# A fused attention and expert kernel: the opening of its first stage in another order

## The chip, the cores and the metric

The kernel runs on one core of one Trainium2 chip. Its time is the device time of one launch, in microseconds (us). The core has five engines that run side by side, each through its own list of instructions: PE (TensorE, matrix products), DVE (VectorE), ACT (ScalarE), POOL (GpSimd) and SP (SyncE, which here only issues transfers). POOL issues transfers as well, on a queue of its own. Engines wait for each other and for transfers by semaphores, and an engine never runs an instruction ahead of an earlier one that still waits.

## The reference

Four layers follow each other, each added to its input: an attention layer whose context is summed by a decaying scan, a layer with 16 experts of which 6 are taken per row, a cross attention under a mask, and a layer with 2 experts of which 1 is taken. Only the first layer and the mask concern this change.

```python
# x: 32 x 56 x 256, ctx_2048: 32 x 1500 x 256, mask: 32 x 1500
def _L0_xattn_ref(Z, kv, decay, W_in, b_in, W_out, b_out, gamma, beta):
    K = jax.nn.sigmoid(decay)
    x = jnp.einsum('btd,ed->bte', kv, W_in) + b_in
    def scan_fn(s, xt):
        s = K * s + xt
        return (s, s)
    _, states = lax.scan(scan_fn, s0, jnp.swapaxes(x, 0, 1))
    proj = jnp.einsum('btd,ed->bte', states, W_out) + b_out
    summary = jnp.mean(proj, axis=1, keepdims=True)
    y = Z + summary
    mu = jnp.mean(y, axis=-1, keepdims=True)
    var = jnp.mean((y - mu) ** 2, axis=-1, keepdims=True)
    return (y - mu) / jnp.sqrt(var + LN_EPS) * gamma + beta
...
x = x + _L0_xattn_ref(_layernorm(x), ctx_2048, ...)
x = x + _L0_ffn_ref(_layernorm(x), ...)                      # 16 experts, 6 per row
x = x + _L1_xattn_ref(_layernorm(x), ctx_2048, mask)         # masked cross attention
x = x + _L1_ffn_ref(_layernorm(x), ...)                      # 2 experts, 1 per row
```

The mean over all states is one weighted sum over the 1500 context rows: row t counts with 1 + K + ... + K^(1499 - t). So the first layer needs, for each of the 32 elements of the batch, one weighted sum of 1500 rows of 256 numbers, and the two weight matrices can be multiplied together once.

## The kernel before, in words

The batch is taken in 16 pairs of elements. A pair's 112 rows of x stand in 128 partitions (56 rows, 8 empty, 56 rows, 8 empty), which is why `xr`, the tile with all rows, is set to zero before the rows are loaded.

**Loads.** Context elements pass through a ring of five slots (`ring`, 1536 KB each). SP loads slots 0 to 4 at the start, with a chunk of four pairs' rows of x (two transfers of 224 KB) after each of the first four. Each call of `count_in(b)` (L315) ends by issuing the load of element b + 5 into the slot that it has read (L331). POOL issues the weights and, last, the mask (L259 to L265), 46.9 KB.

**Constants.** DVE scans the decay into `crow` (L282). Twelve PE products with one column each turn it into columns (`cr`, L292), one more reverses it with `flip` (L299), and DVE copies make `cz`, the weights of the sums (L301 to L306). `count_in(0)` and `count_in(1)` then make the sums of the first pair on PE (L325, 24 products each). PE multiplies the two weight matrices (L341, L349), and makes the bias row and `takes` (L357 to L379). DVE then builds `iota` and the tables `i99` and `om` for the later sort of rows by expert (L389 to L402), and the statistics of the first four pairs (`first_stats(0)`, L425). POOL forms `z` and adds `bet` to `xr` for pairs 0 and 1 (`first_rows(0)`, L432 and L436).

**Mask analysis.** In front of the loop DVE finds for each element where the seen positions begin and whether they fit a window of 384 (L612 to L635): a scan that numbers the positions, two reductions over position times mask, one sign turn of the positions between them, and ten small operations. The results, `starts` and `bad`, are read in the later stages. All its operands lie in parts of `w0_sb`, the tile that later holds the weights of the 16 experts.

**The loop.** Round p does, in this order of issue: `first_norm(p - 1)` and `residual(p - 1)` on DVE (L471 to L479), the sums of pair p, `sum_out` (an ACT copy, L440), the sums into columns (`sp`, PE, and `sv`, DVE, L446 and L451), the projection (`sT`, `sm`, L459 and L463), for pair p - 1 the second normalisation on POOL (`xn`, L491), the turn on PE (L195), the gate (L505) and the choice of experts (`best`, DVE, L516 to L523), and `to_rows(p)` (`bp`, L467), which round p + 1 needs. For earlier pairs it counts places (L537 to L559) and sorts (L571, L593). Rounds 0 to 2 also make four further pairs' statistics (`first_stats(4 * p + 4)`, L425). POOL makes the next `z` and `xr` rows: two pairs in round 0, then one pair a round in the order z, xr, xn. Four buffers hold z, so the fifth z waits until `residual(0)` has used the first.

**What sets the order.** PE, DVE, ACT and SP run their instructions in the order in which the code issues them. In this stage POOL's order is arranged by the framework. After the loop come the 95 expert blocks, the cross attention and the 15 blocks of the last layer, which this change leaves as they are.

The call in question, as it stands in the loop:

```python
            if p >= 1:
                residual(p - 1)
                count_in(2 * p)
                count_in(2 * p + 1)
            sum_out(p)
```

Of the kernel before, what the change touches and what calls it, by code (L numbers as in the profile page):

```python
# [8 lines left out]
F32 = mybir.dt.float32  # L9
U8 = mybir.dt.uint8  # L10
# [3 lines left out]
ALU = mybir.AluOpType  # L14
AX = mybir.AxisListType
# [4 lines left out]
P = 128  # L20
# [39 lines left out]
def xattn_ffn_kernel(  # L60
# [52 lines left out]
    V.tensor_reduce(  # L113
        valid, ident.rearrange("p (h s) -> p h s", s=64)[:, :, 0:S], AX.XY, ALU.add
    )
    row = const.tile([P, 1], F32, name="row")
    V.tensor_reduce(row, before, AX.X, ALU.add)
    V.tensor_scalar(row, row, -1.0, float(P - 1), ALU.mult, ALU.add)
# [14 lines left out]
    V.tensor_scalar(i128, i128, float(P), None, ALU.mult)  # L133

    xr = const.tile([P, NP, D], F32, name="xr")
    G.memset(xr, 0.0)
    gw0_sb = const.tile([P, KD, E0], F32, name="gw0_sb")
    gw1_sb = const.tile([P, KD, E1], F32, name="gw1_sb")
    sel = const.tile([P, NP, E0], F32, name="sel")
# [63 lines left out]


    A.preload_act_table_set("natural_log_exp_and_others")
    w0p = ctx.enter_context(ExitStack())
    w0_sb = w0p.enter_context(tc.tile_pool(name="w0", bufs=1)).tile([P, E0, W0], F32, name="w0_sb")

    def load_w0_up():
        for m, w in ((0, wg0), (1, wu0)):  # L210
# [23 lines left out]
    with tc.tile_pool(name="p1", bufs=1) as p1, tc.tile_pool(name="p3", bufs=3) as p3, tc.tile_pool(  # L234
# [6 lines left out]
        xv = x.rearrange("(p h) s d -> h s p d", h=2)  # L241
        for i in range(NRING):
            load_ctx(i, slots[i])
            if i < 4:
                for h in range(2):
                    nc.sync.dma_start(
                        out=xr[64 * h : 64 * h + S, 4 * i : 4 * i + 4, :],
                        in_=xv[h][:, 4 * i : 4 * i + 4, :],
                    )
        p0 = p1x.enter_context(ExitStack())  # L250
        pw0 = p0.enter_context(tc.tile_pool(name="p0", bufs=1))
# [3 lines left out]
        bout_sb = p1.tile([1, D], F32, name="bout_sb")  # L255
        gam = p1.tile([P, D], F32, name="gam")
        bet = p1.tile([P, D], F32, name="bet")
        for sb, w in ((win_sb, w_in), (wout_sb, w_out), (bin_sb, b_in), (bout_sb, b_out)):
            nc.gpsimd.dma_start(out=sb, in_=w)  # L259
        for sb, w in ((gam, gamma.partition_broadcast(P)), (bet, beta.partition_broadcast(P))):  # L260
            nc.gpsimd.dma_start(out=sb, in_=w)
        for sb, w in ((gw0_sb, gw0), (gw1_sb, gw1)):
            nc.gpsimd.dma_start(out=sb, in_=w)
        mrow = w0_sb[0:B, 4, 0 : T // 4].bitcast(U8)
        nc.gpsimd.dma_start(out=mrow, in_=mask)  # L265

# [16 lines left out]
            crow, kd[:, 3:4].to_broadcast([1, T]), ones[0:1, 0:1].to_broadcast([1, T]), 0.0,  # L283
            ALU.mult, ALU.add,
        )
        ccol = p1.tile([P, NCH], F32, name="ccol")
        cz = p1.tile([P, NCH, Q + 1], F32, name="cz")
        G.memset(cz, 0.0)
# [17 lines left out]
            V.memset(cz[0:q, JM * m + r : JM * m + JM, 1:2], 0.0)  # L306
        sel2 = p1.tile([P, Q], F32, name="sel2")
        V.tensor_reduce(sel2, ident.rearrange("p (g b) -> p b g", b=Q), AX.X, ALU.add)

        pend = {}  # L310

# [74 lines left out]
        for l in range(NL):  # L386
# [7 lines left out]
        V.tensor_reduce(  # L394
            om[:, 1:2], ident.rearrange("p (g o l) -> p g o l", o=2, l=NLP)[:, :, 1, :], AX.XY,
            ALU.add,
        )
        V.tensor_scalar(om[:, 0:1], om[:, 1:2], -1.0, 1.0, ALU.mult, ALU.add)
        for o in range(2):
            V.tensor_scalar(om[:, 2 + o : 3 + o], om[:, o : o + 1], 0.5, -0.5, ALU.mult, ALU.add)  # L400
        for o in (1, 0):
            V.tensor_scalar(  # L402
                i99[:, o, :], i99[:, 0, :], om[:, o : o + 1], om[:, 2 + o : 3 + o], ALU.mult, ALU.add
            )
# [203 lines left out]
        at_t = w0_sb[0:B, 0:2, :].rearrange("p a b -> p (a b)")[:, 0:T]  # L608
        seen = w0_sb[0:B, 2:4, :].rearrange("p a b -> p (a b)")[:, 0:T]
        ends = w0_sb[0:B, 5, 0:4]  # L610
        turns = w0_sb[0:B, 6, 0 : 4 * Q].rearrange("p (i q) -> p i q", q=Q)
        V.memset(turns, 0.0)  # L612
        V.tensor_tensor_scan(
            at_t, ones[0:B, 0:1].to_broadcast([B, T]), ones[0:B, 0:1].to_broadcast([B, T]), 0.0,
            ALU.mult, ALU.add,
        )
        V.tensor_tensor_reduce(
            out=seen, in0=at_t, in1=mrow, scale=1.0, scalar=0.0, op0=ALU.mult, op1=ALU.max,
            accum_out=ends[:, 0:1],
        )  # L620
        V.tensor_scalar(at_t, at_t, -1.0, float(SPAN + 1), ALU.mult, ALU.add)
        V.tensor_tensor_reduce(
            out=seen, in0=at_t, in1=mrow, scale=1.0, scalar=0.0, op0=ALU.mult, op1=ALU.max,
            accum_out=ends[:, 1:2],
        )
        V.tensor_scalar(ends[:, 2:3], ends[:, 1:2], -1.0, float(SPAN), ALU.mult, ALU.add)
        V.tensor_scalar(turns[:, 0, 0:1], ends[:, 2:3], float(LATE), None, ALU.min)
        V.tensor_scalar(
            turns[:, 1, 0:1], ends[:, 0:1], turns[:, 0, 0:1], float(WIN), ALU.subtract, ALU.is_gt
        )  # L630
        for i in range(2):
            V.transpose(out=turns[:, 2 + i, :], in_=turns[:, i, :])
        V.tensor_copy(starts, turns[0:1, 2, :])
        V.tensor_reduce(turns[0:1, 0, 0:1], turns[0:1, 3, :], AX.X, ALU.max)
        V.tensor_copy(bad, turns[0:1, 0, 0:1])  # L635

        def some_pieces(n):
            for _ in range(n):
# [1045 lines left out]
```

## Time and profile before

| what | value |
|---|---|
| median of 3 runs | 731.97 us (731.27 to 733.47) |
| the profiled execution's own time | 731.96 us |
| its span, first to last instruction | 730.3 us |
| mean granted clock of PE | 0.954 |
| busy, whole span: PE, DVE, ACT, POOL | 90%, 55%, 33%, 48% |
| busy, 0 to 15 us: PE, DVE, ACT, POOL | 3.52, 5.62, 1.49, 11.01 us |
| busy, 30 to 45 us: PE, DVE, ACT, POOL | 3.15, 13.94, 1.42, 11.68 us |
| share of the transfer engines, 30 to 45 and 45 to 60 us | 0.97 and 0.67 |
| context moved into the ring | 32 loads of 1536 KB |

The profile lists each instruction with its start, its duration, its engine and its line in the kernel, and for each engine what ended its idle time. "acc<-ring,cz" means that the tile acc was written from the tiles ring and cz. A product in fp32 stands as two records, so 24 products are "x48". PEld is the loading of a product's fixed operand, which runs beside PE. The profile's names leave out numbers: `w_sb` is `w0_sb` here.

### The profile page before, as it was taken

The page shows a single profiled execution, that of the slowest core. Times are in us where ns is not written, and L with a number is a line of the kernel's source. Part 1 is how long each engine was busy: PE and PEld are TensorE (multiplying, and loading weights), DVE is VectorE, ACT ScalarE, POOL GpSimd, SP SyncE. Part 2 cuts the span into 40 slices and gives each one's busy share as a digit, 9 for nine tenths or more (in the row PEclk, how much of TensorE's full clock was granted, in tenths as well). Part 3 has the DMA queues.
Part 4 walks back from the last instruction along what each step waited for, and adds up shares of the span by engine and source line. Part 5 has one row for each costly group of instructions (what it writes and reads, how often), then busy time and mean ns, then how long its engine had stood idle before and what let it go on. Part 6 is the DMA issues. An engine that isn't in the chain of part 4 may idle for free.

```text
span 730.3 us, 13508 instructions
## 1 busy us (share of the span) xinstructions
PE 655.7 (90%) x4099; PEld 438.6 (60%) x4099; DVE 401.3 (55%) x1378; ACT 241.5 (33%) x704; POOL 349.5 (48%) x440
## 2 busy tenths in 40 slices
PE   3558988888779999999999999999988999999996
PEld 3424555555447777667777776666654666666664
DVE  3578687878824655534454447677876232322322
ACT  0113233333214444444444443566551111111110
POOL 6265455554344357667776776568342202112111
PEclk9869799999669999999999999999999999999999
DMA  8969899999716899645554554695941201011000
GB/s 259 316 271 391 316 364 356 369 358 315 214 50 203 265 334 286 206 138 144 153 155 136 157 160 131 185 313 108 332 149 53 69 9 44 25 36 39 26 30 18
DMA packets 70656, 136.62 MB, mean 187 GB/s; under 512 B 7731, under 2 KB 43204, under 8 KB 70580
## 3 DMA queue, kind: packets, MB, share of 16 engines
q1 hardware_dynamic: 56036, 100.31, 39.9%
q0 software_dynamic: 14544, 35.37, 18.0%
q8 instruction: 38, 0.62, 0.4%
q14 instruction: 38, 0.31, 0.1%
HBM read 109.54 MB, written 26.77 MB: 187 GB/s over the span
## 4 chain that ended last, share of the span: by engine, by line
PE 77%; DVE 11%; ACT 3%; POOL 2%; issue 2%; DMA 1%; POOLq 0%; DVEq 0%
PE gu L785 29%; PE y L812 18%; PE acc L325 7%; PE tp L803 5%; PE tp L195 4%; PE tp L913 2%; PE sp L1142 2%; PE owned L593 2%; PE bp L467 1%; PE op L1177 1%; PE lp L505 1%; POOL xn L491 1%; PE sT L459 1%; DVE st L183 1%; ACT xT L197 1%
## 5 line engine op out<-in xcount | busy, mean ns | idle before, releaser
L785 PE MATMUL gu<-w_sb,xT 128*128 x380 | 130.8, 466 | 3.4 <-ACT xT L197 1.9
L791 ACT ACTIVATE sg<-gu 128x176 f32<-128x176 f32 (+1 forms) x155 | 53.1, 343 | 230.3 <-PE gu L785 227.9
L943 POOL DMA_INDIRECT xb<-xn,idx x95 | 91.2, 960 | 63.1 <-PE tp L195 39.7
L785 PE MATMUL gu<-ring,xT 128*128 x240 | 113.7, 597 | 0.0
L797 DVE SCALAR_TENSOR_TENSOR hs<-sg,wgt,gu 128x176 f32<-128x176 f32 x95 | 37.7, 397 | 119.8 <-ACT sg L791 119.8
L812 PE MATMUL y<-w_sb,hT 88*128 x380 | 97.9, 380 | 0.0
L785 PEld LDWEIGHTS gu<-w_sb,xT 128*128 128x128 f32 x380 | 71.5, 191 | 30.7 <-ACT xT L197 2.9
L856 POOL DMA_INDIRECT g<-ys,early x78 | 74.8, 959 | 29.1 <-issue 15.3
L795 DVE TENSOR_TENSOR hs<-sg,gu 128x256 f32<-128x256 f32 x60 | 25.2, 421 | 112.3 <-ACT sg L791 112.3
L1428 POOL DMA_INDIRECT out<-ob,ti x15 | 14.8, 989 | 126.8 <-DVE ob L1425 126.5
L803 PEld LDWEIGHTS tp<-ident,hs 128*88 128x88 f32 (+1 forms) x310 | 40.0, 129 | 57.9 <-issue 46.9
L812 PEld LDWEIGHTS y<-w_sb,hT 88*128 88x128 f32 x380 | 64.5, 190 | 5.7 <-issue 0.6
L785 PEld LDWEIGHTS gu<-ring,xT 128*128 128x128 f32 x240 | 45.6, 192 | 33.3 <-issue 30.4
L805 DVE COPY hT<-tp 88x256 f32<-88x256 f32 (+1 forms) x155 | 64.3, 415 | 0.2 <-PE tp L803 0.2
L812 PE MATMUL y<-ring,hT 128*128 x240 | 61.7, 380 | 0.0
L197 ACT COPY xT<-tp 128x256 f32<-128x256 f32 x126 | 46.9, 372 | 43.4 <-PE tp L195 35.3
L803 PE MATMUL tp<-ident,hs 128*88 128x128 f32 (+1 forms) x310 | 59.2, 273 | 0.0
L325 PE MATMUL acc<-ring,cz 128*32 128x256 f32 x768 | 54.7, 442 | 0.2 <-DVE cz L301 0.2
L951 ACT COPY yb<-y 128x256 f32<-128x256 f32 x95 | 35.3, 372 | 42.8 <-PE y L812 41.9
L432 POOL TENSOR_SCALAR z<-xr,mva,rsa 128x256 f32<-128x256 f32 x16 | 23.0, 1437 | 49.6 <-DVE xr L479 45.4
L195 PE MATMUL tp<-ident,xb 128*128 128x128 f32 x220 | 42.5, 275 | 2.4 <-issue 2.4
L812 PEld LDWEIGHTS y<-ring,hT 128*128 128x128 f32 x240 | 41.0, 190 | 3.3
(307 smaller groups left out, 996.7 us busy)
## 6 DMA issues: line engine op xcount, KB each, us to landing
ring<-in_cx SPq DMA_DIRECT2D x32, 1536.0 KB
ys<-yb SPq DMA_DIRECT2D x95, 128.0 KB
ring<-in_cx SPq DMA_DIRECT2D x16, 384.0 KB
extra<-in_cx SPq DMA_DIRECT2D x16, 384.0 KB
xs<-zrow SPq DMA_DIRECT2D x5, 771.0 KB
w_sb<-in_wg SPq DMA_DIRECT2D x2, 1408.0 KB
w_sb<-in_wu SPq DMA_DIRECT2D x2, 1408.0 KB
xn<-xn SPq DMA_DIRECT2D x16, 128.0 KB
```

The costliest lines, as they stand in the source:

```text
L195: PE.transpose(tp[:, k * P : (k + 1) * P], xn[:, k * P : (k + 1) * P], ident)
L197: A.copy(xT.rearrange("p k c -> p (k c)"), tp[:, 0 : KD * P])
L325: PE.matmul(acc[Q * g : Q * g + Q, 0:D], lhsT=cz[:, j, 1 - h : 1 - h + Q], rhs=c[:, j, :], start=(h == 0 and m == 0), stop=(h == 1 and m = ...
L785: PE.matmul(gu[:, 0 : 2 * fp], lhsT=xT[i][:, k, :], rhs=w[:, bass.ds(at[i] + (u * piece + k * 2 * fp), 2 * fp)], start=(k == 0), stop=(k = ...
L791: A.activation(sg, gu[:, 0:fp], AF.Silu)
L797: V.scalar_tensor_tensor(hs[i, u], sg, wgt[:, i : i + 1], up, ALU.mult, ALU.mult)
L803: PE.transpose(tp[0:h, c * P : (c + 1) * P], a[:, c * h : (c + 1) * h], ident)
L805: V.tensor_copy(hT[i, u], tp[0:h, 0 : 2 * P])
L812: PE.matmul(y[i][:, 0:D], lhsT=a[:, c * P : (c + 1) * P], rhs=w[0:h, bass.ds(at[i] + (u * piece + doff + c * D), D)], start=(u == 0 and c ...
L856: G.indirect_dma_start(out=g, out_offset=None, in_=ys0[0 : n * P, :], in_offset=bass.IndirectOffsetOnAxis(ap=at[:, p, k : k + 1], axis=0),)
L943: G.indirect_dma_start(out=xb, out_offset=None, in_=xn0, in_offset=bass.IndirectOffsetOnAxis(ap=idx[:, i : i + 1], axis=0),)
L951: A.copy(yb, y[:, 0:D])
```

## The change

The arithmetic stays the same; only the order of the beginning changes, and products are added whose result nothing reads.

- The scan that numbers the positions becomes one of DVE's first instructions. The first reduction and the sign turn follow the decay scan, in front of the copies that wait for `cr`. The second reduction and the small operations follow `sel2`, in front of `cs`.
- The mask's transfer is now the first on POOL's queue.
- `xr` is set to zero later, after the other constants, and each chunk of rows is issued one ring load later, so that two context loads go ahead of the first rows.
- Seven products of `ident` with a row of ones, 128 x 512 each, stand at the head of PE's list, in front of `cr`.
- `count_in(2)` and `count_in(3)` move in front of the loop, behind `takes`; round 1 no longer has sums. `sum_out(0)` moves in front of `first_stats(0)`.
- `i99` and `om` are made in round 2, between `first_stats(12)` and `best(1)`.

```diff
@@ after valid
+    at_t = w0_sb[0:B, 0:2, :].rearrange("p a b -> p (a b)")[:, 0:T]
+    V.tensor_tensor_scan(
+        at_t, ones[0:B, 0:1].to_broadcast([B, T]), ones[0:B, 0:1].to_broadcast([B, T]), 0.0,
+        ALU.mult, ALU.add,
+    )
...
     xr = const.tile([P, NP, D], F32, name="xr")
-    G.memset(xr, 0.0)
...
     A.preload_act_table_set("natural_log_exp_and_others")
+    G.memset(xr, 0.0)
...
             load_ctx(i, slots[i])
-            if i < 4:
+            if i > 0:
                 for h in range(2):
                     nc.sync.dma_start(
-                        out=xr[64 * h : 64 * h + S, 4 * i : 4 * i + 4, :],
-                        in_=xv[h][:, 4 * i : 4 * i + 4, :],
+                        out=xr[64 * h : 64 * h + S, 4 * i - 4 : 4 * i, :],
+                        in_=xv[h][:, 4 * i - 4 : 4 * i, :],
                     )
...
+        mrow = w0_sb[0:B, 4, 0 : T // 4].bitcast(U8)
+        nc.gpsimd.dma_start(out=mrow, in_=mask)
         for sb, w in ((win_sb, w_in), (wout_sb, w_out), (bin_sb, b_in), (bout_sb, b_out)):
             nc.gpsimd.dma_start(out=sb, in_=w)
...
-        mrow = w0_sb[0:B, 4, 0 : T // 4].bitcast(U8)
-        nc.gpsimd.dma_start(out=mrow, in_=mask)
@@ behind the scan of the decay (crow)
+        V.memset(turns, 0.0)
+        V.tensor_tensor_reduce(
+            out=seen, in0=at_t, in1=mrow, scale=1.0, scalar=0.0, op0=ALU.mult, op1=ALU.max,
+            accum_out=ends[:, 0:1],
+        )
+        V.tensor_scalar(at_t, at_t, -1.0, float(SPAN + 1), ALU.mult, ALU.add)
+        for i in range(7):
+            warm = ps.tile([P, 512], F32, tag="ps", name="warm")
+            PE.matmul(
+                warm, lhsT=ident, rhs=ones[:, 0:1].to_broadcast([P, 512]), start=True, stop=True
+            )
...
         V.tensor_reduce(sel2, ident.rearrange("p (g b) -> p b g", b=Q), AX.X, ALU.add)
+        V.tensor_tensor_reduce(
+            out=seen, in0=at_t, in1=mrow, scale=1.0, scalar=0.0, op0=ALU.mult, op1=ALU.max,
+            accum_out=ends[:, 1:2],
+        )
...
+        V.tensor_copy(bad, turns[0:1, 0, 0:1])
...
         V.tensor_copy(takes, tk[0:3, 0:P])
+        for b in range(2, 4):
+            count_in(b)
...
-        V.tensor_scalar(i99[:, 0, :], iota[:, 0:NB0], -float(NOT), None, ALU.add)
...
+        def table_constants():
+            V.tensor_scalar(i99[:, 0, :], iota[:, 0:NB0], -float(NOT), None, ALU.add)
...
+        sum_out(0)
         first_stats(0)
         first_rows(0)
...
-        V.memset(turns, 0.0)
...
-        V.tensor_copy(bad, turns[0:1, 0, 0:1])
@@ in the loop
                 residual(p - 1)
+            if p >= 2:
                 count_in(2 * p)
                 count_in(2 * p + 1)
-            sum_out(p)
             if p >= 1:
+                sum_out(p)
                 second_root(p - 1)
...
                 first_stats(4 * p + 4)
+            if p == 2:
+                table_constants()
             if p >= 1:
                 best(p - 1)
```

More of the change, by code (lines that the diff above doesn't have):

```diff
@@ L115, in xattn_ffn_kernel @@
     )
+    w0p = ctx.enter_context(ExitStack())
+    w0_sb = w0p.enter_context(tc.tile_pool(name="w0", bufs=1)).tile([P, E0, W0], F32, name="w0_sb")
+    at_t = w0_sb[0:B, 0:2, :].rearrange("p a b -> p (a b)")[:, 0:T]
[3 more added lines that the diff above has]
+    )
     row = const.tile([P, 1], F32, name="row")
@@ L205, in xattn_ffn_kernel @@
     A.preload_act_table_set("natural_log_exp_and_others")
-    w0p = ctx.enter_context(ExitStack())
-    w0_sb = w0p.enter_context(tc.tile_pool(name="w0", bufs=1)).tile([P, E0, W0], F32, name="w0_sb")
+    G.memset(xr, 0.0)
     def load_w0_up():
@@ L285, in xattn_ffn_kernel @@
         )
+        seen = w0_sb[0:B, 2:4, :].rearrange("p a b -> p (a b)")[:, 0:T]
+        ends = w0_sb[0:B, 5, 0:4]
+        turns = w0_sb[0:B, 6, 0 : 4 * Q].rearrange("p (i q) -> p i q", q=Q)
+        V.memset(turns, 0.0)
[9 more added lines that the diff above has]
+            )
         ccol = p1.tile([P, NCH], F32, name="ccol")
@@ L308, in xattn_ffn_kernel @@
         V.tensor_reduce(sel2, ident.rearrange("p (g b) -> p b g", b=Q), AX.X, ALU.add)
+        V.tensor_tensor_reduce(
+            out=seen, in0=at_t, in1=mrow, scale=1.0, scalar=0.0, op0=ALU.mult, op1=ALU.max,
+            accum_out=ends[:, 1:2],
+        )
+        V.tensor_scalar(ends[:, 2:3], ends[:, 1:2], -1.0, float(SPAN), ALU.mult, ALU.add)
+        V.tensor_scalar(turns[:, 0, 0:1], ends[:, 2:3], float(LATE), None, ALU.min)
+        V.tensor_scalar(
+            turns[:, 1, 0:1], ends[:, 0:1], turns[:, 0, 0:1], float(WIN), ALU.subtract, ALU.is_gt
+        )
+        for i in range(2):
+            V.transpose(out=turns[:, 2 + i, :], in_=turns[:, i, :])
+        V.tensor_copy(starts, turns[0:1, 2, :])
+        V.tensor_reduce(turns[0:1, 0, 0:1], turns[0:1, 3, :], AX.X, ALU.max)
+        V.tensor_copy(bad, turns[0:1, 0, 0:1])
         pend = {}
@@ L391, in xattn_ffn_kernel @@
         i99 = p2.tile([P, 2, NB0], F32, name="i99")
-        V.tensor_scalar(i99[:, 0, :], iota[:, 0:NB0], -float(NOT), None, ALU.add)
         om = p2.tile([P, 4], F32, name="om")
[L394 to L403, printed above, removed]
-            )
+        def table_constants():
+            V.tensor_scalar(i99[:, 0, :], iota[:, 0:NB0], -float(NOT), None, ALU.add)
+            V.tensor_reduce(
+                om[:, 1:2], ident.rearrange("p (g o l) -> p g o l", o=2, l=NLP)[:, :, 1, :], AX.XY,
+                ALU.add,
+            )
+            V.tensor_scalar(om[:, 0:1], om[:, 1:2], -1.0, 1.0, ALU.mult, ALU.add)
+            for o in range(2):
+                V.tensor_scalar(om[:, 2 + o : 3 + o], om[:, o : o + 1], 0.5, -0.5, ALU.mult, ALU.add)
+            for o in (1, 0):
+                V.tensor_scalar(
+                    i99[:, o, :], i99[:, 0, :], om[:, o : o + 1], om[:, 2 + o : 3 + o], ALU.mult, ALU.add
+                )
         vals = p2.tile([P, NE * P], F32, name="vals")
@@ L605, in xattn_ffn_kernel @@
         pieces = list(w0_down_pieces())
[L608 to L611, printed above, removed]
-        V.memset(turns, 0.0)
[L613 to L634, printed above, removed]
-        V.tensor_copy(bad, turns[0:1, 0, 0:1])
         def some_pieces(n):
```

## The prediction

> **What bounds the kernel now.** I began with the busy slices. From 230 us on PE is nine tenths busy and the edit leaves that code alone, so only the first 205 us, the loop over 16 pairs, can move. There I read the windows of 2 us, columns PE, PEld, DVE, ACT, POOL, clock, DMA share, GB/s:
>
> ```profile
> 42.00:44.00 2.00, 1.59 (x4) 0.34 (x4) 1.86 (x11) 0.00 (x0) 2.00 (x2) 0.50 0.87 358
> 44.00:46.00 2.00, 1.55 (x7) 0.62 (x10) 0.45 (x2) 0.77 (x3) 1.75 (x3) 0.50 0.40 158
> 46.00:48.00 2.00, 2.00 (x20) 0.86 (x24) 1.70 (x5) 0.50 (x2) 0.00 (x0) 0.50 0.00 0
> 48.00:50.00 2.00, 1.96 (x32) 0.86 (x24) 0.91 (x3) 0.00 (x0) 1.51 (x2) 0.87 0.13 29
> ```
>
> The transfers run dry for some 5 us: the ring has no free slot because PE has not consumed elements 2 and 3. The waits of the first 60 us say why:
>
> ```profile
> ACT sm L463 <- PE sT L459: 13.6, 3, 10.9
> PE cr L292 <- DVE w_sb L282: 11.5, 1, 11.5
> ...
> PE sT L459 <- DVE sv L451: 8.4, 3, 7.9
> ...
> DVE ccol L297 <- PE cr L292: 5.9, 1, 5.9
> ```
>
> PE waits 7.9 us for one tiny DVE copy (sv), and everything behind it waits too. The chain of waits names what stood in front of it (start, duration, what):
>
> ```profile
> 39.01 1.73 DVE w_sb L622 x2
> ...
> 42.22 0.15 DVE sv L451
> ...
> 44.73 1.22 PE bp L467 x2
> 45.95 4.06 PE acc L325 x48
> ...
> 54.41 2.73 PE acc L325 x48
> ...
> 63.02 4.06 PE acc L325 x48
> ```
>
> So the mask analysis (L612 to L635, 32.53 to 42.2) sits on the path. After it the loop is no transfer problem: adding up the trace's DMA packets by queue, each context load lands 10 to 18 us before its sums from element 4 on. A round is a latency chain, DVE first_norm and residual, POOL z, xr and xn, PE turn, gate and bp, of 9.2 us (94.99, 104.19, 113.37 in the chain). Hence time won before round 2 reaches the end.
>
> **What the skill says.** "TensorE: Matmul & The Clock Gate", Part 1: the array's clock is half by default, full after a busy window of about 3.4 us, and the windows run free. The trace agrees: 48 products of L325 take 4.06 us at clock 0.50 and 2.73 at 1.00. The first clock event is at 21.2 us; before it the page prints 1.00, but the 40 products from 19.13 on run at the slow pace, so I take PE as slow until then. "SBUF — State Buffer", section on two separate sides: a DVE operation with two SBUF inputs and a POOL operation that reads SBUF exclude each other. The trace agrees: under the scan of L613 (to 35.84) the first z took 3.56 us, later ones 1.21:
>
> ```profile
> 32.63 3.21 DVE L613 TENSOR_TENSOR_SCAN w_sb<-ones 32x1500 f32<-32x1500 f32 x1
> ...
> 33.31 3.56 POOL L432 TENSOR_SCALAR z<-xr,mva,rsa 128x256 f32<-128x256 f32 x1 [4.20 <-ACT rsa L190]
> ```
>
> "DMA: Bandwidth & Descriptors", "Issuing engines are not separate DMA queues": POOL's and SP's transfers interleave on the same 16 engines; so they do here, the mask's packets ending between 17.1 and 20.5 us among the ring's.
>
> **The change, step by step.** Times of after carry a prime; sums are against the profiled execution, 731.96 us (span 730.3), which is the runs' median, 731.97.
>
> 1. Position scan first on DVE. It runs 1.83' to 5.05' (3.21 us as L613). POOL's affine_select for "before" reads SBUF, so by the lock it slips from 2.1' to 5.05'; the row reduction starts at 5.4' against 5.44 now. The decay scan ends at 11.3 as now. Price 0, hidden in DVE's 3.62 us wait; gain 0. The other end, no lock: 0.4 us gained and step 3 starts 3 us sooner.
>
> 2. Context before rows, and xr's memset later. Behind the affine_select the 3.50 us memset ends at 8.85'. SP holds two ring loads before the first rows, 3072 KB, which at before's pace land by about 14', so the engines have work until SP is released. Bytes are equal. Element 3 is preceded by two row chunks instead of three and lands near 29' (30.5 now). Rows come one chunk later: about 17', 24', 31', 37', needed at about 29', 32', 38', 55'. Price 0.
>
> 3. Mask first on POOL's queue. Issue 8.9'. The first POOL transfer now takes 2.85 us from issue (5.72) to first packet (8.57); so 11.8', landed about 12.4'. The weights issue 3.2 us later, from 9.4'; w_in lands about 14', its use is at 21'. The last of the nine waits for the mask to land, then come flip and cz.
>
> 4. Mask analysis in DVE's waits. The first reduction follows the landing: 12.4' + 1.97 + 1.17 for the sign turn = 15.5', then ccol. The rest, 1.73 + 1.5 us, stands before cs, idle now from 19.6 to 25.6. Flip's select is locked out until 15.5', ready 15.8'.
>
> 5. Seven unread products. One 128x512 fp32 product took 2.06 us at half clock (L583, 193.86) and four halves 1.88 at full, so 0.94. From 1.6' at 2.0 us until the gate opens (one full window, 4.2' to 7.6'), then 0.94: end 9.6' to 11.4', under DVE's scan. The 12 ones-column products (24 records, 5.73 us, 239 ns) then run at full clock; L446, also 128 wide weights, falls from 252 to 152 ns, so 24 x 0.15 = 3.6 us: 11.4' to 15.1'. If the gate has closed again: 17.1'.
>
> 6. Up to the sums. cf starts at about 16.2' (ccol and flip, step 4) against 17.57: 1.3 us won. The first pair and the weight products keep their length, so "takes" starts at 26.9' against 28.16.
>
> 7. Table constants leave the path: i99 and om (28.86 to 30.28) give 1.4 us. First statistics end at 29.8', z may start at 30.5' against 33.31.
>
> 8. Second pair ahead of round 0. PE: 26.8' to 30.5' (element 3 lands 29'), then sp 0.6, sv 0.2, sT 1.0, sm 0.4, bp 0.7: 33.6'. first_norm and residual of pair 0 end about 36'. No mask analysis stands before sv.
>
> 9. POOL is late next. In its order come z, z, xr, xr, z, z, xr, xr, z, xr, xn: five z at 1.21, five xr at 0.71, one xn at 1.22, with gaps 11 us, free of the scans that stretched it before: 30.5' to 41.5'. It covers 2.4 us of step 8.
>
> 10. Round 1 ends: PE has been idle, so half clock: tp 0.69, copy 0.4, lp 1.03, bp 1.15: 44.9'. That stands against 54.41 now: 9.5 us won.
>
> 11. Paid back. The sums of pair 2 run cold, 4.06 instead of 2.73 us, and sv waits for them: first_norm(2) loses 1.4. DVE's part of round 2 from sv to the last statistics is 5.0 us without a gap, and the constants, 1.4 us, now stand between it and best(1); of those 0.7 were slack in which DVE waited for ACT's lg, and first_norm(1) no longer waits 0.4 for best(0). So first_norm(2) starts at 57.7' against 64.81: **7.1 us won**. Later rounds keep 9.2 us plus the clock's drops, which cost now some 4 us between 79 and 155; I take the same.
>
> 731.97 - 7.1 = 724.9, say **725 us**. Unknowns and both ends: mask landing 10' (cf then 15.3': +0.9) to 15' (ccol 18.2': -2.6); products all cold -5.4, gate open through the first pair +1.4; pair 2 warm +1.4; phase of the clock windows later on -2 to +2.
>
> **Rivals.** *Products stay cold.* 1.6' + 7 x 2.0 = 15.6', cr until 21.3' (5.73), 4.1 later than now in place of 1.3 sooner: 7.1 - 5.4 = 1.7 us won, 730. For it: the 24 small records of L292 filled a window and opened nothing. Against: in the 2 us windows the dense sums from 45.9 opened the gate by 48.5.
>
> *The mask is late* (slower). DVE takes work in order, so behind L617's reduction stand ccol, cz and all sums. Landing at t gives ccol at t + 3.1; cf is later than 16.2' by t - 12.9, the gain is 20 - t, and the sign turns at t = 20. Slower by 2.2 us beyond 22; at 23 it is 735. For it: now the packets end at 20.5, 8.1 us after issue, with 830 KB ahead of them in that queue. Against: they are now first; even 8.1 us gives 17 and 729.
>
> *The transfers become the bound.* If the loop hangs on loads, only the dry spell comes back: the missing shares from 44 to 52 sum to 5.6 us, 726.4. For it: DMA share 1.01 from 120 to 150. Against: leads of 10 to 18 us; PE waited once for a load, 0.7 us.
>
> *Warm and lucky.* Flip unlocked, pair 2 warm, two clock drops fewer: 7.1 + 1.3 + 1.4 + 1.5, 721.
>
> **How the numbers follow.** Central sum 0.60 (own range 722.5 to 727), warm and lucky 0.11, transfers 0.07, a mask around 17 or half-cold products (727 to 729.5) 0.10, cold products 0.07, mask beyond 20 0.05. Range 720.5 to 729.5: the last two cases and the tails lie outside. 0.3%, 2.2 us, is about what a measurement tells here. Faster 0.87 (the first four, less a little), same 0.08, slower 0.05.
>
> **What would show it.** Sums of elements 2 and 3 near 27' to 31' with a wait for the ring in front of the latter; cr halves of 0.15 us; POOL without a gap from 30.5' to 41.5'; pair 2 at about 45' at half clock; DMA never at 0 near 46'; then rounds of 9.2 us. Wrong would be: the mask reduction starting after 15', products of 2 us to the end, POOL's z above 1.3 us, PE waiting for the ring inside the loop, or new half-clock stretches in most rounds.

## The result and the profile after

The changed kernel takes 726.91 us in the median of four runs (726.26 to 727.44), the kernel before beside it 731.91 us (731.27 to 733.47): a ratio of 0.9926, interval 0.9901 to 0.9951; the quotient of the two medians is 0.9932, well within it. The forecast was 725.0 us. A second set of runs of the same pair gave 727.51 against 733.09 us, 0.9936 (0.9915 to 0.9957). The profiled execution has a span of 725.2 us against 730.3, at the same mean clock of 0.954.

Of the 5.1 us of span, 4.8 are there when the sums of the last pair end (175.0 us after the start against 179.8; here and below this end is the start of their last product). So the front of the loop decides, as assumed. How much of it was won is seen at three marks:

| mark | before | after | won | forecast |
|---|---|---|---|---|
| first z of POOL starts | 33.31 | 33.93 | -0.6 | 2.8 |
| sums of pair 2 start | 54.34 | 48.20 | 6.1 | 9.5 |
| first_norm(2) starts | 64.81 | 60.20 | 4.6 | 7.1 |
| end of all sums | 179.8 | 175.0 | 4.8 | |

First, windows of 2 us of the kernel after, around the time at which the transfers of the kernel before ran dry (columns: PE, PEld, DVE, ACT, POOL, clock, transfer share, GB/s):

```profile
44.00:46.00 2.00, 0.69 (x2) 0.29 (x2) 0.00 (x0) 0.34 (x2) 0.88 (x1) 0.50 1.04 414
46.00:48.00 2.00, 1.92 (x6) 1.43 (x6) 0.56 (x5) 0.78 (x5) 0.00 (x0) 0.50 0.97 387
48.00:50.00 2.00, 2.00 (x21) 0.89 (x24) 1.77 (x6) 0.72 (x4) 0.00 (x0) 0.50 0.88 361
50.00:52.00 2.00, 2.00 (x36) 0.98 (x28) 1.09 (x3) 0.00 (x0) 1.27 (x2) 0.76 0.58 200
```

In these windows the share falls to 0.58 once and never to 0.00. DVE, which in the kernel before was at the mask analysis from 32.5 to 42.2, is idle between 44 and 46. The clock is at half until 51.

The waits of the first 60 us (who waited for whom: total, times, longest) no longer have PE's 7.9 us for sv. The largest that bear on the opening are these:

```profile
DVE ccol L317 <- PE cr L312: 3.2, 1, 3.2
...
PE cr L312 <- DVE w_sb L295: 2.9, 1, 2.9
...
PE bp L505 <- DMA sm<-cvec: 2.3, 1, 2.3
```

The chain of waits of the kernel after (start, duration, what) says where the time went that was to be won earlier, and what stands in round 1:

```profile
2.06 3.04 POOL before L106
...
6.18 2.40 DVE ids L135
...
9.85 3.27 DVE w_sb L288
13.12 0.15 DVE w_sb L295
13.27 5.74 PE cr L312 x24
...
30.72 6.21 DMA sm<-cvec
...
37.07 0.96 PE bp L505 x2
...
41.66 1.20 POOL z L470
42.95 0.72 POOL xr L474
43.67 1.22 POOL xn L529
...
44.93 0.70 PE tp L201 x2
...
48.27 4.08 PE acc L360 x48
```

Two things differ from the forecast. The decay scan (L288) starts at 9.85, not at 8.06 as before; in front of it stands `ids`, an operation on 16 numbers a partition that takes 2.40 us (0.23 in the kernel before). And the products of `cr`, with the unread products in front of them, take 5.73 us as before, not 3.6. The timeline of the kernel after shows `ids` and its neighbours:

```profile
2.02 3.07 POOL L106 TENSOR_SCALAR_AFFINE_SELECT before<-before 128x128 f32<-128x128 f32 x1
...
5.05 3.50 POOL L212 MEMSET xr<- 128x4096 f32 x1
...
6.18 2.40 DVE L135 TENSOR_SCALAR ids<-e,row 128x16 f32<-128x16 f32 x1
6.32 2.26 DVE L137 TENSOR_TENSOR_SCAN i<-ones 1x15 f32<-1x15 f32 x1
...
8.50 0.73 POOL L264 DMA_DIRECT2D w_sb<-in_mask  x1
```

The position scan holds the affine_select until 5.05, as step 1 said (3.07 us against 0.28 in the kernel before). That pushes the zeroing of `xr` to 5.05 to 8.55, and `ids` and the small scan behind it both end at 8.58, when the zeroing ends. The row that showed the lock before, the first z, is now free of it (two z in 2.44 us; before, one took 3.56):

```profile
33.93 2.44 POOL L470 TENSOR_SCALAR z<-xr,mva,rsa 128x256 f32<-128x256 f32 x2 [2.70 <-DMA xr<-in_x]
```

Five of the runs below (e5 to e8, and e12) took 45 to 49 us more than the others, the kernel before beside them too, nearly all of it behind the last sums and in code that no edit touches; why stays open.

### The profile page after: what moved, and what is told of

Its sections match the earlier page's. It is cut to its first block, busy times and chain, and to the rows that moved or that the text cites. A ratio compares the mean times of both kernels' runs of the same rounds, so it can differ in the third digit from the quotient of the medians.

```text
span 725.2 us, 13538 instructions
## 1 busy us (share of the span) xinstructions
PE 662.7 (91%) x4113; PEld 441.0 (61%) x4113; DVE 402.1 (55%) x1378; ACT 241.8 (33%) x704; POOL 348.7 (48%) x440
## 4 chain that ended last, share of the span: by engine, by line
PE 79%; DVE 11%; POOL 3%; ACT 3%; issue 2%; DMA 2%; POOLq 0%; DVEq 0%
PE gu L798 29%; PE y L825 18%; PE acc L360 7%; PE tp L816 5%; PE tp L201 4%; PE tp L926 2%; PE sp L1155 2%; PE owned L631 2%; PE op L1190 1%; PE bp L505 1%; PE lp L543 1%; DVE st L189 1%; POOL xn L529 1%; DVE oh L609 1%; DMA sm<-cvec 1%
## 5 line engine op out<-in xcount | busy, mean ns | idle before, releaser
L798 PEld LDWEIGHTS gu<-w_sb,xT 128*128 128x128 f32 x380 | 71.5, 192 | 30.6 <-ACT xT L203 2.9
L816 PEld LDWEIGHTS tp<-ident,hs 128*88 128x88 f32 (+1 forms) x310 | 39.9, 130 | 58.7 <-issue 46.7
L360 PEld LDWEIGHTS acc<-ring,cz 128*32 128x32 f32 x768 | 27.4, 124 | 24.0 <-issue 11.6
```

What stands on the lines that cost most here:

```text
L360: PE.matmul(acc[Q * g : Q * g + Q, 0:D], lhsT=cz[:, j, 1 - h : 1 - h + Q], rhs=c[:, j, :], start=(h == 0 and m == 0), stop=(h == 1 and m = ...
L798: PE.matmul(gu[:, 0 : 2 * fp], lhsT=xT[i][:, k, :], rhs=w[:, bass.ds(at[i] + (u * piece + k * 2 * fp), 2 * fp)], start=(k == 0), stop=(k = ...
L816: PE.transpose(tp[0:h, c * P : (c + 1) * P], a[:, c * h : (c + 1) * h], ident)
```

## The experiments

The times are compared as ratios to the runs of before beside them, the beginnings by the trace. e11 is the change itself, run once more: both marks come 0.8 us later than in the first trace, because the clock rose to full at 25.4 us in place of 23.7 under the first sums. A difference of that size between two traces is therefore not read as the effect of an edit.

| run | edit | pair 2's sums start | all sums end | ratio (interval) |
|---|---|---|---|---|
| before | | 54.3 | 179.8 | 1 |
| after | | 48.2 | 175.0 | 0.9926 (0.9901, 0.9951) |
| e11 | after once more | 49.0 | 175.7 | 0.9936 (0.9915, 0.9957) |
| e1 | xr zeroed early | 47.6 | 173.4 | 0.9912 (0.9889, 0.9936) |
| e2 | no unread products | 49.4 | 176.1 | 0.9927 (0.9905, 0.9950) |
| e3 | second pair back in round 1 | 47.3 | 174.9 | 0.9899 (0.9868, 0.9930) |
| e4 | mask analysis back | 53.0 | 179.1 | 0.9988 (0.9972, 1.0005) |
| e5 | bias row without the transfer | 49.2 | 175.8 | 0.9920 (0.9895, 0.9946) |
| e6 | xn of pair 0 on DVE | 46.8 | 172.4 | 0.9943 (0.9918, 0.9968) |
| e7 | products in round 1 | 46.9 | 173.6 | 0.9908 (0.9871, 0.9944) |
| e8 | five edits at once | 44.4 | 167.4 | 0.9829 (0.9795, 0.9863) |
| e10 | e8, decay first | 48.2 | 173.4 | 0.9899 (0.9876, 0.9922) |
| e12 | e10, second pair back | 42.1 | 165.4 | 0.9834 (0.9787, 0.9881) |

### Which part of the change carries the gain: e4, e3, e2

e4 puts the whole mask analysis back in front of the loop; the mask's transfer stays first, and everything else stays changed.

```diff
@@ behind valid
-    V.tensor_tensor_scan(
-        at_t, ones[0:B, 0:1].to_broadcast([B, T]), ones[0:B, 0:1].to_broadcast([B, T]), 0.0,
-        ALU.mult, ALU.add,
-    )
@@ behind the decay scan, and behind sel2
-        V.memset(turns, 0.0)
...
-        V.tensor_copy(bad, turns[0:1, 0, 0:1])
@@ in front of the loop
         first_rows(0)
+        V.tensor_tensor_scan(
...
+        V.tensor_copy(bad, turns[0:1, 0, 0:1])
```

> The changed kernel with the whole mask analysis back in front of the loop; the mask's transfer stays first. Theory 1 (the analysis in front of sv was what held the loop back): sv(0) comes some 8 us later, POOL's z are stretched by the scan again, the sums of pair 2 start at about 54 us instead of 48.2, 731 to 733 us; the decay scan starts sooner, by up to 2 us, since no scan holds POOL's select. Rival (the gain is the early sums of the second pair): the time stays below 729.

Measured: 0.9988, no difference from before. The waits of e4's first 60 us:

```profile
PE sT L468 <- DVE sv L460: 9.8, 3, 9.3
```

The wait for sv is back, longer than before (9.3 against 7.9 us), since pair 0's sp runs sooner (30.56 against 33.52) and sv still stands behind the analysis. And so is the dry spell, in e4's windows:

```profile
52.00:54.00 2.00, 2.00 (x14) 0.89 (x18) 1.65 (x8) 0.55 (x3) 0.00 (x0) 0.50 0.32 94
54.00:56.00 2.00, 2.00 (x28) 0.88 (x24) 1.73 (x6) 0.50 (x2) 0.53 (x1) 0.52 0.03 8
```

So the ring ran dry because the round hung on sv, not because the second pair's sums came late. e3 tests the reverse: only the sums of elements 2 and 3 go back.

```diff
-        for b in range(2, 4):
-            count_in(b)
...
-            if p >= 2:
+            if p >= 1:
                 count_in(2 * p)
```

> The changed kernel with the sums of elements 2 and 3 back in round 1. Theory 1 (round 1 ends with POOL's eleven operations, from 33.9 to 44.9 us, and PE is idle under them): the sums fit under POOL's work, their price is nothing or up to 1 us, 726.9 to 728. The ring goes dry again for some microseconds and that costs nothing either. Rival (having the second pair's sums early is what gives the gain): most of the 5.0 us is lost, 730 to 732.

Measured: 0.9899, not slower than the change; sums of pair 2 at 47.3, sooner by 0.9 us. Pair 1's sums stand at 38.24 in PE's idle time behind bp of pair 0, and the clock is at full from 41.2 to 48. Against the expectation, the ring does not run dry either: the lowest share between 36 and 54 is 0.76. The early sums of the second pair give nothing, and the rival in which they carry the gain falls.

e2 takes the seven unread products out.

```diff
-        for i in range(7):
-            warm = ps.tile([P, 512], F32, tag="ps", name="warm")
-            PE.matmul(
-                warm, lhsT=ident, rhs=ones[:, 0:1].to_broadcast([P, 512]), start=True, stop=True
-            )
```

> The changed kernel without the seven unread products. Theory 1 (the products opened the gate from 6.6 to 13.4 us and closed again before cr began at 13.27): the 24 records of cr take 5.73 us as before, all else stays, 726.9 us within 0.7 either way. Rival (the products are what makes the opening quick): cr or the first sums become slower and the time rises by 2 us or more, to 729 or above.

Measured: 0.9927, the ratio of the change itself. The products of cr start at 13.27 and take 5.73 us in both, as e2's timeline has it:

```profile
13.27 5.73 PE L307 MATMUL cr<-ones,w_sb 1*128 1x1 f32 x24 [13.27 <-DVE w_sb L295]
```

The sums of pair 1 start 0.9 us later, but so they do in e11, which has the products. So the gain needs the mask analysis out of the way (e4), and not the early sums (e3) or the unread products (e2). The order of the rows, the table constants and sum_out(0) were not taken out one by one; together with the rest they give nothing that e4 can tell from zero, but whether they matter once the analysis is gone is not shown.

### What the early part lost: e1 and e9

e1 zeroes `xr` early, as the kernel before does.

```diff
     xr = const.tile([P, NP, D], F32, name="xr")
+    G.memset(xr, 0.0)
...
     A.preload_act_table_set("natural_log_exp_and_others")
-    G.memset(xr, 0.0)
```

> The changed kernel with the memset of xr back at its old place in the code, so that POOL runs it from 1.7 us, beside DVE's position scan, and not from 5.05 to 8.55. Theory 1 (POOL's memset held DVE's small operation on ids for 2.2 us, so the decay scan began at 9.85 instead of 8.06 us): ids takes 0.23 us again, the decay scan begins at about 8.1 us, everything behind it is 1.8 us sooner, 725.1 us; if the gate of the clock is still open for the first 2 us of the twelve products, up to 1.1 us more, 724.0. Theory 2 (the opening is held by transfers: the bias row sm takes 6.2 us to land and bp waits for it): the time stays at 726.9 within 0.5.

Measured: 0.9912, within the interval of the change; the times can't tell the two. The timeline of e1 can:

```profile
1.65 3.50 POOL L143 MEMSET xr<- 128x4096 f32 x1
...
6.48 0.23 DVE L135 TENSOR_SCALAR ids<-e,row 128x16 f32<-128x16 f32 x1
...
8.05 3.27 DVE L288 TENSOR_TENSOR_SCAN w_sb<-kd,ones 1x1500 f32<-1x1500 f32 x1
...
38.57 1.79 DVE L516 SCALAR_TENSOR_TENSOR z<-z,mv,gam 128x256 f32<-128x256 f32 x1
38.68 1.39 POOL L474 TENSOR_TENSOR xr<-xr,bet 128x256 f32<-128x256 f32 x2
```

With the zeroing out of its way `ids` is back at 0.23 us and the decay scan at 8.05: 1.8 us won there, and 1.4 at the first z (32.49). Of these only 0.6 reach the sums of pair 2, less than two traces of one kernel differ by. The bias row lands late (bp at 36.2), and then DVE's residual, two operands from SBUF, meets POOL's two sums of xr and takes 1.79 us in place of 0.48. All sums end 1.6 us sooner than in the change.

e9, which ran once and serves for the pace of cr alone, asks why these products didn't become faster. In e1 they started at 11.47 with the clock granted at 1.00, and still each record took 0.233 us.

```diff
-                lhsT=crow[:, o : o + P * JM].rearrange("o (p j) -> o j p", j=JM)[:, j % JM, :],
+                lhsT=crow[:, o + P * (j % JM) : o + P * (j % JM) + P],
```

> The changed kernel, but the twelve products that turn the decay into columns read 128 consecutive numbers of crow each, not every fourth one (so the context rows get the wrong weights; all else runs as it does). In the changed kernel and in the one with the early zeroing these products kept 0.233 us a record under a granted clock of 1.00 and of 0.50 alike. T1 (the step through the row sets their pace): under 0.15 us a record, 3.6 us in all or less. T2 (a product with a one-row operand of 128 columns costs this much however it is read): 0.233 us again, 5.7 us.

Measured: 4.27 us, neither of the two numbers, and the reason is visible. First e1's windows (every fourth number read), then e9's (consecutive numbers), columns as above; in these windows PE has little else than cr:

```profile
11.00:12.00 1.00, 0.53 (x3) 0.56 (x3) 1.00 (x3) 0.00 (x0) 0.40 (x1) 1.00 1.02 387
12.00:13.00 1.00, 1.00 (x6) 1.00 (x5) 1.00 (x2) 0.00 (x0) 1.00 (x4) 0.69 1.01 328
```

```profile
13.00:14.00 1.00, 0.73 (x7) 0.77 (x7) 1.00 (x3) 0.00 (x0) 1.00 (x4) 1.00 0.97 328
14.00:15.00 1.00, 1.00 (x8) 1.00 (x8) 0.96 (x3) 0.00 (x0) 1.00 (x4) 0.67 1.04 406
15.00:16.00 1.00, 1.00 (x6) 1.00 (x6) 0.86 (x1) 0.00 (x0) 0.06 (x2) 0.50 1.02 401
```

In e9 the first nine records start 0.11 us apart (13.27 to 14.15), and from the drop of the clock at 14.3 on the starts are 0.21 us apart. Read consecutively, the pace follows the clock. Read with a step of four it stays at 0.233 us under either clock. And the gate of the clock (open at 1.00, closed at 0.50), which the unread products had opened, does not stay open for them: PE counts as busy throughout, and the clock drops. In e1 it is at half from 12.4 to 22.6, though cr's products keep PE busy until 17.2.

### What sets the end of round 1: e5, e6, e7

e5 takes the bias row's transfer out of pair 0's path.

```diff
-            PE.matmul(bp[:, 0:D], lhsT=takes, rhs=sm, start=True, stop=True)
+            if p == 0:
+                PE.matmul(bp[:, 0:D], lhsT=takes[0:2], rhs=sm[0:2], start=True, stop=False)
+                PE.matmul(bp[:, 0:D], lhsT=ones[0:1, :], rhs=cvec, start=False, stop=True)
+            else:
+                PE.matmul(bp[:, 0:D], lhsT=takes, rhs=sm, start=True, stop=True)
```

> The changed kernel, but pair 0 gets its bias row by a second product of PE (a row of ones by cvec) and so does not wait for the transfer of sm, which landed at 36.93. T1 (POOL's chain of z, xr and xn sets the end of round 1, as step 9 had it): bp of pair 0 at 35.0 to 35.3 in place of 37.07, residual(0) some 1.9 us sooner, and yet xn of pair 0 stays at 43.7, the sums of pair 2 at 48.2, and the time at 726.9. T2 (the late transfer of step 8 sets it): xn and all behind it 1.9 us sooner, 725.0.

e6 makes xn of pair 0 on DVE.

```diff
-            (V if p == NP - 1 else G).tensor_scalar(
+            (V if p in (0, NP - 1) else G).tensor_scalar(
```

> The changed kernel, but DVE, not POOL, makes xn of pair 0, so that this row no longer stands behind the 11 us of z and xr on POOL. T1 (POOL's chain sets the end of round 1): xn at about 41.7, tp of pair 0 behind sT at 43.3 in place of 44.93, sums of pair 2 at 46.6, first_norm(2) 1.6 us sooner, 725.3. T2 (POOL's chain is cover only; the transfer or PE's own chain sets the end): nothing moves, 726.9. xn may be stretched on DVE beyond its 0.4 us while POOL works, up to 1.2 us.

Measured, in e5's timeline, then in e6's:

```profile
34.81 2.44 POOL L470 TENSOR_SCALAR z<-xr,mva,rsa 128x256 f32<-128x256 f32 x2 [2.71 <-ACT rsa L196]
...
36.10 0.69 PE L506 MATMUL bp<-sm,takes 2*128 2x256 f32 x2 [0.45 <-ACT sm L501]
...
44.62 1.22 POOL L533 TENSOR_SCALAR xn<-xr,mv 128x256 f32<-128x256 f32 x1
```

```profile
42.20 0.67 DVE L529 TENSOR_SCALAR xn<-xr,mv 128x256 f32<-128x256 f32 x1 [0.53 <-ACT mv L196]
...
43.52 0.69 PE L201 MATMUL tp<-ident,xn 128*128 128x128 f32 x2
...
46.79 0.20 PEld L360 LDWEIGHTS acc<-ring,cz 128*32 128x32 f32 x8 [0.65 <-issue]
```

In e5 the first z starts 0.9 us later than in the change (34.81, as in e11), and yet bp 1.0 us sooner; but xn follows 9.8 us behind the first z, as in the change (33.93 to 43.66, 9.7). The transfer was hidden behind POOL's chain. In e6 tp (the turn on PE) comes at 43.52 (43.3 expected) and the sums of pair 2 at 46.79 (46.6 expected), all sums 2.6 us sooner. That settles it: POOL's chain ends last in round 1. The ratio of e6 (0.9943) doesn't show the 2.6 us; its interval is 0.25% to either side, 2 us, so what of the gain reached the end stays open.

e7 is to keep the gate open with six more unread products, two each in front of bp of pair 0, and of sp and tp of round 1.

```diff
+        def unread(n):
+            for _ in range(n):
+                PE.matmul(
+                    owned.rearrange("p c l -> p (c l)"), lhsT=ident,
+                    rhs=ones[:, 0:1].to_broadcast([P, 512]), start=True, stop=True,
+                )
...
+            if p == 1:
+                unread(2)
             sum_in_columns(p)
...
+            if p == 1:
+                unread(2)
             if p >= 1:
                 turned(p - 1)
...
+            if p == 0:
+                unread(2)
             to_rows(p)
```

> The changed kernel with six more products of 128 x 512 that nothing reads, in PE's waits of round 0 and round 1: two in front of bp of pair 0, two in front of sp and two in front of tp of round 1. T1 (round 1 and the sums of pair 2 pay for the half clock between 37.3 and 51.0): the gate stays open, lp 0.62 in place of 1.04, bp 0.69 in place of 1.22, sums of pair 2 2.8 in place of 4.14 and 1.2 sooner, first_norm(2) at 57.9 in place of 60.2, 724.6. T2 (later rounds give it back, since the clock drops again at the next wait of PE): first_norm(2) sooner, time within 1 us of 726.9.

Measured: half of it. lp (the products of the expert gate) takes 0.62, bp 0.69 and pair 2's sums start at 46.94, as expected. But PE was busy for only 0.73 us between 44 and 46, and the clock falls 0.5 us behind the start of the sums, as e7's windows show:

```profile
44.00:46.00 2.00, 0.73 (x5) 0.44 (x5) 0.00 (x0) 0.63 (x3) 0.81 (x1) 1.00 1.03 412
46.00:48.00 2.00, 2.00 (x22) 1.24 (x25) 1.22 (x8) 0.72 (x4) 0.00 (x0) 0.86 0.94 375
48.00:50.00 2.00, 2.00 (x26) 0.94 (x20) 1.76 (x5) 0.50 (x2) 0.20 (x1) 0.50 0.89 364
```

So the sums take 4.48 us, not 2.80, first_norm(2) starts at 59.26 (57.9 expected, 60.20 in the change), and the ratio of 0.9908 is within the change's interval.

### The head start as one chain: e8, e10, e12

e8 joins e1, e5, e6 and four of e7's products (none in front of bp), and makes the table constants in round 1, where DVE idles.

```diff
-            if p == 2:
+            if p == 1:
                 table_constants()
```

> All at once on the changed kernel: xr set to zero early again, the bias row of pair 0 by a product, xn of pair 0 on DVE, two unread products in front of sp and two in front of tp of round 1, table constants in round 1 where DVE idles. T1 (the head start is one chain, and each of these shortens it): bp of pair 0 at 34.5, tp at 39.5, sums of pair 2 at about 41 to 42 and at full clock, first_norm(2) at 52 to 54, 720 with 3 to either side. T2 (something later, the transfers or the rounds of 9.2 us, takes the gain): sums of pair 2 sooner, but from pair 4 on PE waits for the ring, and 724 or more.

Measured: 0.9829, clear of the change's interval. Pair 2's sums start at 44.38 and take 2.80 us, and all sums end at 167.4, 7.6 us before the change's. Some three microseconds more were expected there, and the unread products took them: two, at half clock, held sp until 38.76 though ACT's copy for it was done at 37.4, and two more held tp until 42.37 though xn was ready at 39.9 and sT done at 40.6. In e8's timeline of PE:

```profile
35.31 3.66 PE L540 MATMUL owned<-ones,ident 128*128 128x512 f32 x4
38.76 0.56 PE L484 MATMUL sp<-sel,acc 128*128 128x2 f32 x4
```

The first eight loads land no sooner than in the change, and PE waits for one of them once (element 3, 0.64 us); they had not set the change's time.

e10 adds the decay at the head of DVE's list to e8, with both reductions behind sel2, flip early, no unread products in front of cr, and xr zeroed by ACT.

```diff
+    flip = w0_sb[:, 15, 0:P]
...
+    kd = const.tile([1, 4], F32, name="kd")
+    nc.sync.dma_start(out=kd[:, 0:1], in_=decay)
...
+    V.tensor_tensor_scan(
+        crow, kd[:, 3:4].to_broadcast([1, T]), ones[0:1, 0:1].to_broadcast([1, T]), 0.0,
+        ALU.mult, ALU.add,
+    )
+    A.activation(
+        xr.rearrange("p a d -> p (a d)"), ones[:, 0:1].to_broadcast([P, NP * D]), AF.Copy, scale=0.0
+    )
     at_t = w0_sb[0:B, 0:2, :].rearrange("p a b -> p (a b)")[:, 0:T]
...
-    G.memset(xr, 0.0)
```

> The kernel with all five edits at once (e8_all), and the decay made first: its small operations and scan at the head of DVE's list, the scan of positions behind it, both reductions behind sel2, flip made early on POOL, xr set to zero by ACT, no unread products in front of cr. T1 (the head start is one chain from the decay to the sums of pair 2): decay scan from 4.3 to 7.6, cr at 7.8, first sums at 14.8, sums of elements 2 and 3 at 25 and 27.4 (the latter behind its load), sums of pair 2 at about 41, some 3 us less than e8_all, a ratio to the kernel before of about 0.979. T2 (the loads hold the sums): a wait for the ring of over 3 us in front of the sums of pair 1 or 2, and no gain on e8_all.

> The changed kernel once more, for a comparison on one chip with e10_decay_first: a ratio to the kernel before of 0.9926 as measured, give or take 0.3%, if the gain doesn't depend on the chip.

Measured: first sums at 13.67, 4.7 us sooner than in e8, and yet 0.9899, against 0.9936 for the change beside it. The timeline of e10:

```profile
24.49 1.50 PE L355 MATMUL acc<-ring,cz 128*32 128x256 f32 x24
30.61 2.79 PE L355 MATMUL acc<-ring,cz 128*32 128x256 f32 x24 [4.62 <-DMA ring<-in_cx]
33.33 1.02 PE L479 MATMUL sp<-sel,acc 128*128 128x2 f32 x4
...
36.92 1.22 PE L501 MATMUL bp<-sm,takes 2*128 2x256 f32 x2 [0.45 <-ACT sm L496]
```

PE waits 4.62 us for element 3, and pair 0's sp, which needs nothing of it, stands behind that wait. The clock falls to half meanwhile (at 29.1), so what follows is slow as well. This is the price of putting the second pair's sums in front of round 0: nothing in the change, where the load had landed at 28.8, 2.7 us ahead, and the whole gain here, where PE is ready sooner but the load lands at 30.6. e12 puts them back, and also takes out the two unread products in front of sp of round 1.

```diff
-        for b in range(2, 4):
-            count_in(b)
...
-            if p >= 2:
+            if p >= 1:
                 count_in(2 * p)
...
-            if p == 1:
-                unread(2)
             sum_in_columns(p)
```

> e10_decay_first with the sums of the second pair back in round 1, behind residual(0), and without the two unread products in front of sp of round 1. In e10 the sums of element 3 waited 4.6 us for their load, and sp and bp of pair 0 stood behind them on PE. T1 (that wait, put in front of pair 0's own path by the early sums, ate what the early decay had won): bp of pair 0 at about 28 in place of 37, sums of pair 1 still at 30.6 behind their load but with nothing behind them that pair 0 needs, sums of pair 2 at 40 to 42 in place of 48.2, end of all sums some 6 us sooner than in e10, ratio to the kernel before about 0.981. T2 (the loads hold every round): sums of pair 2 wait for the ring too, and the ratio stays near 0.990.

The timeline of e12:

```profile
29.43 1.22 PE L499 MATMUL bp<-sm,takes 2*128 2x256 f32 x2 [0.45 <-ACT sm L494]
30.45 1.06 PE L500 MATMUL bp<-cvec,ones 1*128 1x256 f32 x2
31.43 4.48 PE L355 MATMUL acc<-ring,cz 128*32 128x256 f32 x48
...
42.07 2.80 PE L355 MATMUL acc<-ring,cz 128*32 128x256 f32 x48
```

bp of pair 0 comes 7.5 us sooner, the sums of pair 1 wait for no load, and all sums end at 165.4, 8.0 us before e10's and 9.6 before the change's. At most 1.5 us of this belongs to the two products that were taken out: in e10 they held sp until 42.49, though ACT's copy for it was done at 41.01. The ratio is 0.9834. e8 and e12 both beat the change; which of the two is faster their intervals don't tell.

## Why the prediction was right, and where its steps were off

The sign, the place and the carrier were right: the analysis of the mask stood between sp and sv, and with it put back the whole gain is gone (e4). The size was 2 us short: 7.1 us forecast, 5.1 measured.

**Step 1, price 0: wrong, 1.8 us.** The lock was applied in one direction: the scan that holds POOL's affine_select. What it shifts was missed: step 2 let the zeroing of xr end at 8.85 and named nobody beside it. It lay on DVE's `ids`, and on the decay scan behind it. "SBUF — State Buffer" of the Trainium skill, in the section on two separate sides, has the missing half: the lock goes to whichever starts first, and a POOL operation holds it against a DVE operation in its two-port mode as well. The trace agrees where POOL only writes (`ids` 2.40 us under the zeroing in the change and 0.23 in e1), though the small operations in front of `ids`, one number a partition, ran beside the same zeroing at 0.15 us each, and a scan of 16 numbers a partition at 0.18. Which DVE operations are held was read from these few, not tested. e4, with the zeroing in its late place but started sooner, has the same hold (2.41 us).

**Step 2**, the order of transfers, and **step 3** held: the mask's last packet ended at 11.45 and its landing was signalled at 12.09 (12.4 forecast), and its reduction ran right behind the scan without a wait. The slower rival, a late mask, had no ground.

**Step 5: the products end at 10.35 as forecast, but the saving on cr (2.1 us) did not come.** Two assumptions failed. The speed of L446's products was carried over to products with one-row operands, whose pace with a step of four in the operand is 0.233 us at clock 1.00 and 0.50 (e1, e9). And the gate closed again at 13.4, when cr had just begun at 13.27. The rival "products stay cold" was priced too high: at half clock a product started every 1.71 us here, not every 2.0, so seven of them would have ended near 13.5 (an estimate, 1.57 + 7 x 1.71), 0.3 us after cr began in the change, and cr's own pace would have been what it was.

**Step 6** followed: cf (the reversed columns) at 19.35, not 16.2. With 1.8 us from step 1 and 2.1 from step 5, less the wait for the mask that step 4 had allowed for, the 3.1 us are covered. Step 7's 1.4 us for the table constants came, but the first z started 3.4 us later than forecast (33.93 against 30.5), the same delay.

**Step 8 was mis-sized.** bp of pair 0 began at 37.07, 1.9 us after sm's other two rows were there (35.2): the third row's transfer, 1 KB, took 6.21 us from issue. The forecast had not priced it at all. "DMA: Bandwidth & Descriptors" of the Trainium skill, section "Anatomy of one DMA", puts the fixed cost of a transfer at about 2.0 us; here, with the transfer share at 1.05, the whole took three times that. It cost nothing, since **step 9 was right**: POOL worked from 33.93 to 44.88 without a gap, 10.95 us against the 11 forecast, and e5 and e6 show that this chain, not the transfer, ended last. In e1, where z starts sooner, POOL does wait, 1.02 us, for residual(0) behind that bp.

**Step 10** gives 48.2 in place of 44.9: the same 3.3 us. Its half clock was right (lp 1.04, bp 1.22). **Step 11** was too pessimistic: the payback is 1.5 us (6.1 to 4.6), not 2.4. Its own terms, 1.4 for the half clock, 0.7 for the constants and 0.4 back, add up to 1.7, not 2.4. The half clock in pair 2's sums came as priced (4.14 us against 2.80), the constants cost 0.7, and 0.5 came back elsewhere than forecast: DVE's part from sv to the last statistics took 4.6 us in place of 5.0, for the most part because one cast (`qi`) took 0.17 us where it had taken 0.65 beside POOL's sum of xr.

So the error of 3.3 us from steps 1 and 5 met, by luck, 0.9 us of payback forecast too much, and 2.5 us are missing at first_norm(2). Later rounds kept 9.2 us plus clock drops, and the gain at the start of each pair's sums stayed between 3.8 and 6.8 us.

**The rivals.** "Transfers become the bound" gave 726.4, closer to the result than the forecast, by chance: in the change what reads the ring waits for a load once, 0.3 us, and e8, whose first eight loads land no sooner, ends the sums 7.6 us sooner. The leads of 10 to 18 us were counted in packets; a landing is signalled some 2 us after the last packet (element 3 in the change: 28.8 and 26.6). "Warm and lucky" did not occur.

## What to carry to other kernels

When an operation is moved, follow the one that it displaces, and ask of that one too whom it holds: the cost here was not in the moved scan, nor in what it held, but in the zeroing that slid onto DVE's path. Before spending instructions on the clock, see in the trace that the products to be sped up do follow the clock. A step in front of a queue is free only as long as everything that it waits for has arrived; in e10 the same move that was free in the change cost all that a faster start had won.

## What the runs showed of the hardware

- A POOL memset, which reads nothing, held a DVE operation of 128 x 16 fp32 from SBUF to SBUF for 2.2 us (2.40 against 0.23), while operations of 128 x 1 and a scan of 128 x 16 beside it ran at 0.15 and 0.18. ACT's zeroing of the same 4096 numbers a partition took 3.60 us (e10), and DVE's operations on one number beside it took 0.14 to 0.18 us, the scan of the decay 3.27 as elsewhere; `ids` did not run beside it.
- POOL's sums held DVE too: an operation on two tiles took 1.79 in place of 0.48 us beside two of them (e1). Beside POOL's z alone the same operation took 0.51 (the change). The other way round, DVE's scan of the positions held POOL's affine_select: 3.07 us in the change, 0.28 in e4, where the scan stands elsewhere.
- Products with a one-row operand of 128 fp32 numbers: 0.233 us a record with a step of four, at clock 1.00 and 0.50; 0.11 and 0.21 us when read consecutively.
- A transfer of 1 KB took 6.21 us from issue to landing while the transfer engines were fully loaded (share 1.05); in the other traces it took 6.0 to 6.8.
- In the change the gate opened 5.0 us after the start of the first unread product (1.57 to 6.6) and closed 3.1 us after the end of the last (10.35 to 13.4). In the ten traces with these products in front of cr it opened between 4.7 and 7.7 us, and stayed open for 6.8 us in each.
